# Values projected in the routing pass, slot lists built by VectorE beside four rounds, gate with tokens on partitions: one change to a fused attention and mixture-of-experts kernel

## The chip, the cores and the metric

The kernel runs on one core of a Trainium2 chip. The metric is the device time of one execution in microseconds, the median of several runs. All data is float32.

## The reference: what is computed

For 4096 tokens (4 sequences of 1024) of width H = 256:

```
xn  = layernorm(x)
out = x + attention(xn) + moe(xn)
attention: q, k, v = xn @ w.T, 16 heads of 16
  local  = causal linear attention with elu(q)+1, elu(k)+1, in chunks of 128 tokens
  coarse, fine = reads of four memories per head by elu(q)+1
  gprob  = sigmoid(relu(coarse @ eg_w1.T + b1) @ eg_w2.T + b2)      # one per token
  output = (gate*(gprob*fine + (1-gprob)*coarse) + (1-gate)*local) @ w_o.T
moe: logits = xn @ gate_weight.T (8 experts), softmax, top 2, weights renormalised
  y = sum over the 2 chosen experts of weight * swiglu_expert(xn), plus a shared swiglu expert
```

An expert is 176 wide, the shared one 352. A token's two experts are found first; then rows of `xn` are gathered expert by expert.

## The kernel before

**Tiles.** Tokens come in 32 tiles of 128 (`NTT`), four to a block (`NT = 4`), eight blocks (`NBLK`). `xnT` holds a block's normalised tokens with channels on partitions; every projection reads it. For the experts, the 8192 (token, choice) pairs are sorted by expert and packed into `NST = 71` slots of 128 rows, each slot belonging to one expert.

**Order.** Nothing is scheduled by the compiler: `manual_schedule` keeps the order in which Python calls the functions, and each engine runs its own instructions in that order. A *unit* is (weight, function, arguments). `mix` interleaves several lists of units in proportion to the weights, `split` cuts a list into parts of like weight, `run` emits. So a weight only places a unit; it is no time. The PSUM has the four banks of `quad` and a rotation of four single banks, `bank(...)`.

**Stages, in the order they are emitted (L1102 to L1152):**

1. *Routing*: a software pipeline over the blocks: `statistics` (VectorE), three steps later `normalize` (VectorE one tile, ScalarE three, then SP stores the block to `xns` in DRAM), one more step later `transpose_x` (TensorE, copied by ScalarE), one more `logits`. Only six blocks of `x` fit in SBUF (`AHEAD`), so the loads of blocks 6 and 7 are issued behind the stores of blocks 0 and 1. `logits` multiplies each token tile with 128 columns of `wvg` (values and gate weights side by side, 264 columns) and keeps the last eight. The queries of blocks 0 and 1 are projected here too. `route(0)` chooses the experts of the first half. After the loop SP copies `x` to `sums` in DRAM.
2. *Sorting and the head* (L1129 to L1144): one `mix` of `sorting` with block 0's keys and values, its shared expert, and attention rounds 0 and 1. `sorting` is `route(1)`, `sort`, `slots`, `weights`: VectorE chains on small tiles; then the slot lists: 22 batches of `invert` (one-hots of three columns of pairs: `places`, position within a slot, and `tiles`, number of the slot; GpSimd multiplies `tiles` with token numbers and with weights into `held`) each followed by `add_slots` (TensorE: `found += places.T @ held`); then `inverted` (writes `islot`, `wslot`) and `owners`.
3. *Rounds 2 to 29*: each is a `mix` of `attention_round(n)`, a quarter of the projections of a later block (`beside`: keys, values, queries, shared expert of blocks 1 to 7, spread over rounds 0 to 27), and 1/28 of `experts()` (`side`). A round scores and masks tile n (`scores`, `mask`), transposes and writes out tile n-2 (`output`), reads the memories (`memory`, `weigh`, `fine`), computes the gate of tile n-1 (`gate_hidden`, `gate_out`) and the local attention (`local`, `back`, `update`). A slot takes `fetch` (GpSimd gathers rows of `xns`, SP loads the weights), `expert_in`, `expert_hidden`, `expert_turn`, `expert_out`, and `put` (GpSimd issues a DMA that adds the result to `sums`).
4. *Tail*: rounds 30 to 33 with `totals`, which read `sums` back and write `out`.

**The gate before.** `gate_hidden` puts the 64 hidden channels on partitions (`w1` stationary, tokens streaming), ScalarE adds the bias and applies Relu, and `gate_out` multiplies by `w2` in one column on TensorE (L840) ahead of the Tanh.

Of the kernel before, what the change touches and what calls it, by code (L numbers as in the profile page):

```python
# [22 lines left out]
def linear_attention_moe_kernel(  # L23
# [51 lines left out]
    AHEAD = 6  # L75
# [10 lines left out]
    big = ctx.enter_context(tc.tile_pool(name="big", bufs=AHEAD))  # L86
# [13 lines left out]
    def bank(name):  # L100
        return ps_r.tile([P, 512], FP, tag="r", name=name)


    def load_x(blk):
        xb = big.tile([P, NT, H], FP, tag="tok", name=f"x_{blk}", bufs=AHEAD)
        nc.sync.dma_start(
            xb, x[blk * TB : (blk + 1) * TB, :].rearrange("(n p) h -> p n h", p=P)
        )
        st["x", blk] = xb

    for blk in range(AHEAD):
        load_x(blk)
# [18 lines left out]
    b1 = const.tile([HID, 1], FP, tag="b1", name="b1")  # L131
    nc.scalar.dma_start(b1, eg_b1)
    w2 = const.tile([HID, 1], FP, tag="w2", name="w2")
    nc.scalar.dma_start(w2, eg_w2)
# [169 lines left out]
    def normalize(blk):  # L304

        xb = st["x", blk]
        mv, rstd = st.pop(("norm", blk))
        shift = small.tile([P, NT], FP, tag="shift", name=f"shift_{blk}")
        nc.vector.scalar_tensor_tensor(
            shift, mv[:, :, 0], -1.0, rstd, ALU.mult, ALU.mult  # L310
        )
        xnT = io.tile([P, NC, TB], FP, tag="xnT", name=f"xnT_{blk}")
        st["xnT", blk] = xnT
        nc.vector.tensor_scalar(
            xb[:, NT - 1, :], xb[:, NT - 1, :], mv[:, NT - 1, 0:1], rstd[:, NT - 1 : NT],
            ALU.subtract, ALU.mult,
        )
        for i in range(NT - 1):
            nc.scalar.activation(
                xb[:, i, :], xb[:, i, :], AF.Identity,  # L320
                bias=shift[:, i : i + 1], scale=rstd[:, i : i + 1],
            )
        nc.sync.dma_start(
            xns[blk * TB : (blk + 1) * TB, :].rearrange("(n p) h -> p n h", p=P), xb
        )
        if blk + AHEAD < NBLK:
            load_x(blk + AHEAD)

# [13 lines left out]
    def logits(blk):  # L342

        xnT = st["xnT", blk]
        pl = bank(f"pl_{blk}").rearrange("p (i e) -> p i e", i=NT)
        for i in range(NT):
            for k in range(NC):
                nc.tensor.matmul(
                    pl[:, i, :], xnT[:, k, i * P : (i + 1) * P], wvg[:, k, H + E - P : H + E],
                    start=(k == 0), stop=(k == NC - 1),  # L350
                )
        nc.scalar.copy(lgs[:, blk * NT : (blk + 1) * NT, :], pl[:, :, P - E :])
# [134 lines left out]
    def invert(lo):  # L487
# [3 lines left out]
        if lo == 0:  # L491
            st["found"] = bank("found")
        n = min(3, 2 * NTT - lo)
        some = slice(lo, lo + n)
# [3 lines left out]
        tiles = ones_at[:, n * P : n * (P + NST)].rearrange("p (n s) -> p n s", s=NST)  # L498
        nc.vector.tensor_tensor(
            tiles, count[:, None, :NST].to_broadcast([P, n, NST]),  # L500
            lohi[:, 1, some, None].to_broadcast([P, n, NST]), ALU.is_equal,
        )
        nc.vector.tensor_tensor(
            places, count[:, None, :P].to_broadcast([P, n, P]),
            lohi[:, 0, some, None].to_broadcast([P, n, P]), ALU.is_equal,
        )
        held = exw.tile([P, 2 * H], FP, tag="wdn", name=f"held_{lo}")
        held = held[:, : n * 2 * NST].rearrange("p (n v s) -> p n v s", v=2, s=NST)
        for v, what in enumerate((token, two)):
            nc.gpsimd.tensor_mul(  # L510
                held[:, :, v], tiles, what[:, some, None].to_broadcast([P, n, NST])
            )
# [53 lines left out]

    def values(blk, i):
        xnT = st["xnT", blk]
        if i == 0:
            wide = att.tile([P, NT, NH * D1 + CW - D1], FP, tag="va", name=f"va_{blk}")  # L570
            nc.gpsimd.memset(wide[:, :, NH * D1 :], 0.0)
            va = wide[:, :, : NH * D1].rearrange("p i (h k) -> p i h k", k=D1)
            nc.gpsimd.memset(va[:, :, :, HD:D1], 1.0)
            st["va", blk] = va
            st["wide", blk] = wide
        pv = bank(f"pv_{blk}_{i}")
        for k in range(NC):
            nc.tensor.matmul(  # L578
                pv[:, :H], xnT[:, k, i * P : (i + 1) * P], wvg[:, k, :H],
                start=(k == 0), stop=(k == NC - 1),  # L580
            )
        nc.scalar.copy(
            st["va", blk][:, i, :, :HD],
            pv[:, :H].rearrange("p (h k) -> p h k", k=HD),
        )
# [239 lines left out]
    def gate_hidden(n):  # L825

        cT = st.pop(("cT", n))
        ph = bank(f"ph_{n}")
        for c in range(NC):
            nc.tensor.matmul(  # L830
                ph[:HID, :P], w1[:, c, :], cT[:, c, :], start=(c == 0), stop=(c == NC - 1)
            )
        h1 = tmp.tile([HID, P], FP, tag="h1", name=f"h1_{n}")
        nc.scalar.activation(h1, ph[:HID, :P], AF.Relu, bias=b1)
        st["h1", n] = h1

    def gate_out(n):

        pz = bank(f"pz_{n}")
        nc.tensor.matmul(pz[:, :1], st.pop(("h1", n)), w2, start=True, stop=True)  # L840
        prob = small.tile([P, 1], FP, tag="prob", name=f"prob_{n}")
        nc.scalar.activation(prob, pz[:, :1], AF.Tanh, bias=b2, scale=0.5)
# [166 lines left out]
    first_round, last_round = 2, 30  # L1009
# [12 lines left out]
    def run(units):  # L1022
        for _, f, *args in units:
            f(*args)

    def keys_values(blk):
        units = [(1024, project, blk, wk, c, False) for c in range(NC)]
        return units + [(512, values, blk, i) for i in range(NT)]
# [10 lines left out]
    def projections(blk):  # L1039

        units = keys_values(blk) + (queries(blk + 1) if blk + 1 < NBLK else [])
# [28 lines left out]
    def experts():  # L1070
        units = [(1, fetch, 0), (1, fetch, 1), (128, expert_in, 0)]
# [31 lines left out]
    for s in range(NBLK + 5):  # L1103
# [8 lines left out]
        if 0 <= s - 5 < NBLK:  # L1112
            routing += [(256, logits, s - 5)]
        if s == NBLK:
            routing += [(64, memories_by_group)]
        if s == NBLK + 1:
            routing += [(256, route, 0)]
        if NBLK <= s < NBLK + 2 * BPB:
            blk, c = divmod(s - NBLK, NC)
            routing += [(1024, project, blk, wq, c, True)]  # L1120
# [8 lines left out]
    sorting = [(2000, route, 1), (1800, sort), (100, shift_logits), (3200, slots)]  # L1129
    sorting += [(2400, weights)]  # L1130
    batches = list(range(0, 2 * NTT, 3))
    for k, lo in enumerate(batches):
        sorting += [(200, invert, lo)]
        sorting += [(400, add_slots, batches[k - 1])] if k else []
    sorting += [(400, add_slots, batches[-1]), (64, inverted), (1200, owners)]
    start = keys_values(0)
    start[4:4] = [(64, living), (64, mean_queries, 0), (64, gates_of_heads)]
    start += [(64, batch_weights, 0), (32, odd_keys, 0)]
# [3 lines left out]
    head = [u for n in range(first_round) for u in rounds[n]]  # L1142
    head = mix(head, shared(0) + [u for n in range(first_round) for u in beside[n]])
    run(mix(sorting, start + head))  # L1144
# [64 lines left out]
```

## Time and profile before

| | us |
|---|---|
| three runs | 776.08, 778.08, 779.90 |
| median of them | 778.08 |
| the profiled execution, its own time | 782.79 |
| its span, first to last instruction | 781.1 |

| engine | busy us | share of the span | instructions |
|---|---|---|---|
| PE (matmul) | 700.7 | 90% | 5268 |
| PEld (weight load) | 491.0 | 63% | 5268 |
| DVE (VectorE) | 426.1 | 55% | 1084 |
| ACT (ScalarE) | 273.8 | 35% | 707 |
| POOL (GpSimd) | 400.3 | 51% | 441 |

How to read it: a group's row has line, engine, operation, output<-inputs, shape, count, then busy time and the mean duration of one, then idle time of the engine just before it and what ended it. A float32 matmul is recorded as two instructions, so x4 in the chain stands for two calls. "Chain" is the work that ended last, followed back from the end. A stretch of the windows view gives, for 20 us, the busy time of each engine, the clock that TensorE was granted (1.00 is full) and the share of the DMA engines.

### The profile page before, as it was taken

The numbers are of one execution on the slowest core, as the hardware profiler recorded it, in microseconds if no ns is written. First come the engines' busy times: TensorE is split into PE (matmuls) and PEld (weight loads), VectorE is DVE, ScalarE is ACT, GpSimd is POOL, SyncE is SP. The second block draws the span as 40 slices with busy tenths as digits, with TensorE's granted clock in tenths as the row PEclk, the third lists the DMA queues.
The fourth block names the chain that finished last, engine by engine and source line by source line (L and its number), as shares of the span: only waits on it lengthen the run. The fifth ranks groups of instructions, "written<-read, shape, count | busy, mean of one in ns | idle before, by whom it ended". The sixth has DMA issues, their size and how long they took to land.

```text
span 781.1 us, 14630 instructions
## 1 busy us (share of the span) xinstructions
PE 700.7 (90%) x5268; PEld 491.0 (63%) x5268; DVE 426.1 (55%) x1084; ACT 273.8 (35%) x707; POOL 400.3 (51%) x441
## 2 busy tenths in 40 slices
PE   1798579499999999999999999999999999999965
PEld 0675356366676666666667667666766667767653
DVE  6536857445446744455536644554457555655553
ACT  2563002123443333433443343433443344334300
POOL 3100366506555656464546555556545646657576
PEclk9899689889999999999999999999999999999976
DMA  9554000234343453344444443443443444454285
GB/s 283 183 178 134 1 0 1 59 107 97 84 117 85 90 118 84 86 106 94 97 111 92 103 104 84 93 113 84 97 104 85 107 101 103 108 123 99 29 261 171
DMA packets 86373, 81.48 MB, mean 104 GB/s; under 512 B 7437, under 2 KB 83901, under 8 KB 86173
## 3 DMA queue, kind: packets, MB, share of 16 engines
q1 hardware_dynamic: 69661, 59.64, 26.5%
q0 software_dynamic: 13632, 18.62, 14.3%
q10 hardware_dynamic: 3008, 2.28, 0.9%
q8 instruction: 42, 0.69, 0.4%
q14 instruction: 30, 0.25, 0.1%
HBM read 62.56 MB, written 22.15 MB: 108 GB/s over the span
## 4 chain that ended last, share of the span: by engine, by line
PE 76%; DVE 7%; DMA 5%; POOL 4%; ACT 3%; issue 3%; SPq 0%; POOLq 0%; DVEq 0%; ACTq 0%
PE phe L968 12%; PE pye L991 8%; PE po L895 5%; PE psu L871 5%; PE pg L856 5%; PE quad L658 4%; PE pn L684 4%; PE po L899 3%; PE pv L578 3%; PE pq L550 3%; PE pk L550 3%; PE quad L770 3%; PE pxg L959 2%; PE pTe L982 2%; PE ph L830 2%
## 5 line engine op out<-in xcount | busy, mean ns | idle before, releaser
L1000 POOL DMA_INDIRECT sums<-y,islot x71 | 112.7, 1588 | 81.0 <-DMA sums<-y,islot 29.9
L792 POOL TENSOR_TENSOR cg<-coarse,gates 128x256 f32<-128x256 f32 x32 | 23.7, 742 | 165.1 <-DVE coarse L785 164.9
L968 PE MATMUL phe<-wgu,xgT 128*128 128x352 f32 x284 | 100.9, 478 | 1.1 <-ACT hTe L984 0.9
L665 DVE TENSOR_TENSOR sT<-quad,causal 128x512 f32<-128x512 f32 x128 | 80.2, 682 | 14.3 <-PE pk L736 6.5
L933 POOL DMA_INDIRECT xg<-xns,islot x71 | 71.3, 1005 | 15.9 <-issue 8.8
L991 PE MATMUL pye<-wdn,hTe 88*128 88x256 f32 x284 | 76.6, 392 | 1.8 <-ACT oT L822 1.0
L968 PEld LDWEIGHTS phe<-wgu,xgT 128*128 128x128 f32 x284 | 49.9, 191 | 25.3 <-issue 5.3
L810 POOL TENSOR_TENSOR fm<-fm 128x512 f32<-128x512 f32 x32 | 43.6, 1363 | 36.5 <-DVE prob L843 23.1
L974 DVE SCALAR_TENSOR_TENSOR the<-the,phe 128x176 f32<-128x176 f32 x71 | 23.8, 335 | 69.6 <-ACT the L973 66.8
L991 PEld LDWEIGHTS pye<-wdn,hTe 88*128 88x128 f32 x284 | 49.5, 189 | 15.1 <-issue 5.5
L995 ACT ACTIVATE y<-pye,wslot 128x256 f32<-128x256 f32 x71 | 33.6, 473 | 58.6 <-PE pye L991 55.7
L895 PE MATMUL po<-wd,h 128*128 128x256 f32 (+1 forms) x192 | 49.2, 394 | 0.0
L973 ACT ACTIVATE the<-phe 128x176 f32<-128x176 f32 x71 | 22.5, 318 | 74.5 <-PE phe L968 72.5
L871 PE MATMUL psu<-xnT,wu 128*128 128x512 f32 (+1 forms) x96 | 47.6, 620 | 0.0
L856 PE MATMUL pg<-xnT,wg 128*128 128x512 f32 (+1 forms) x96 | 47.0, 613 | 0.7 <-ACT nT L691 0.7
L799 DVE TENSOR_TENSOR fm<-quad,rw 128x512 f32<-128x512 f32 x64 | 42.0, 682 | 0.0
L863 DVE SCALAR_TENSOR_TENSOR th<-th,pg 128x512 f32<-128x512 f32 (+1 forms) x24 | 16.4, 684 | 43.8 <-ACT th L862 39.6
L876 DVE SCALAR_TENSOR_TENSOR h<-th,psu 128x512 f32<-128x512 f32 (+1 forms) x24 | 16.5, 686 | 42.9 <-PE psu L871 42.2
L961 ACT COPY xgT<-pxg 128x256 f32<-128x256 f32 x71 | 26.5, 373 | 37.1 <-PE pxg L959 18.3
L895 PEld LDWEIGHTS po<-wd,h 128*128 128x128 f32 (+1 forms) x192 | 36.1, 200 | 4.3
L558 DVE SCALAR_TENSOR_TENSOR sqT<-pq,eq 128x512 f32<-128x512 f32 x16 | 11.1, 692 | 50.8 <-ACT eq L556 50.7
L563 DVE SCALAR_TENSOR_TENSOR skT<-pk,ek 128x512 f32<-128x512 f32 x16 | 11.1, 691 | 49.8 <-ACT ek L556 47.1
(195 smaller groups left out, 1510.2 us busy)
## 6 DMA issues: line engine op xcount, KB each, us to landing
wgu<-in_w_gate_dram SPq DMA_DIRECT2D x71, 176.0 KB
wgu<-in_w_up_dram SPq DMA_DIRECT2D x71, 176.0 KB
wdn<-in_w_down_dram SPq DMA_DIRECT2D x71, 176.0 KB
x<-in_x_dram SPq DMA_DIRECT2D x8, 512.0 KB
xns<-x SPq DMA_DIRECT2D x8, 512.0 KB
sums<-in_x_dram SPq DMA_DIRECT2D x8, 512.0 KB
part<-sums SPq DMA_DIRECT2D x14, 256.0 KB
out_dram<-acc SPq DMA_DIRECT2D x14, 256.0 KB
```

Source lines behind the costliest of these rows:

```text
L550: nc.tensor.matmul(pq, w[:, k, c * P : (c + 1) * P], xnT[:, k, :], start=(k == 0), stop=(k == NC - 1),)
L665: nc.vector.tensor_mul(sT, quad[:, g, :].rearrange("p (c t) -> p c t", t=P), causal[:, None, :].to_broadcast([P, NC * 2, P]),)
L799: nc.vector.tensor_mul(fm[:, c].rearrange("p g m (r k) -> p g (m r) k", k=HD), quad[:, :, c * KM + KX + KN : (c + 1) * KM].rearrange("p g ...
L810: nc.gpsimd.tensor_add(fm[:, :, 0:2, :], fm[:, :, 0:2, :], fm[:, :, 2:4, :])
L856: nc.tensor.matmul(pg[:n, :], wg[:, k, f * P : f * P + n], xnT[:, k, :], start=(k == 0), stop=(k == NC - 1),)
L871: nc.tensor.matmul(pu[:n, :], wu[:, k, f * P : f * P + n], xnT[:, k, :], start=(k == 0), stop=(k == NC - 1),)
L895: nc.tensor.matmul(po[:, :H], st["h", blk, f][:k, tok], wd[:k, f, :], start=(f == 0), stop=False)
L933: nc.gpsimd.indirect_dma_start(out=xg, out_offset=None, in_=xns, in_offset=bass.IndirectOffsetOnAxis(ap=islot[:, j : j + 1], axis=0),)
L968: nc.tensor.matmul(ph[:, : 2 * F], xgT[:, k, :], wgu[:, k].rearrange("p g f -> p (g f)"), start=(k == 0), stop=(k == NC - 1),)
L991: nc.tensor.matmul(py[:, :H], hT[:, f, :], wdn[:, f, :], start=(f == 0), stop=(f == 1))
L995: nc.scalar.activation(y, py[:, :H], AF.Copy, scale=wslot[:, j : j + 1])
L1000: nc.gpsimd.indirect_dma_start(out=sums, out_offset=bass.IndirectOffsetOnAxis(ap=islot[:, j : j + 1], axis=0), in_=st.pop(("y", j)), in_of ...
```

## The change

Five edits that hang together:

- *Values in the routing.* `logits` is gone; `values` runs in its place for all eight blocks, two token tiles at a time, with all 264 columns of `wvg` into `quad`. ScalarE copies 256 columns to the values and eight to `lgs`. The values overwrite the block's own `x` tile, which is made wider (`VW`), so there are eight such tiles and all eight loads are issued at once (no `AHEAD`); the copy into it must wait for the block's store to `xns`. `keys_values` becomes `keys`. The queries of blocks 0 and 1 leave the routing.
- *normalize*: VectorE two tiles, ScalarE two (was one and three).
- *invert*: per column three `tensor_scalar` on VectorE: `places` by is_equal, and each half of `held` by is_equal and multiply in one instruction. GpSimd has no part in it.
- *Order*: sorting is mixed with the queries of blocks 0 and 1, block 0's keys and shared expert only. Then rounds 0 to 3 run with `beside` and the slot lists (`owners` first, `add_slots` two batches behind `invert`), and `fetch` 0 and 1 at their end. `first_round` is 4, so the experts are spread over 26 rounds instead of 28.
- *Gate*: tokens on partitions. The coarse tile is stationary and `w1` (64 columns) streams; VectorE adds the bias, then does Relu, multiply by `w2` and the sum in one instruction with an accumulator. The one-column matmul and ScalarE's Relu are gone.

```diff
-        xb = big.tile([P, NT, H], FP, tag="tok", name=f"x_{blk}", bufs=AHEAD)
+        wide = big.tile([P, NT, VW], FP, tag="tok", name=f"x_{blk}")
+        xb = wide[:, :, :H]
...
-    for blk in range(AHEAD):
+        st["wide", blk] = wide
+    for blk in range(NBLK):
         load_x(blk)
...
-    def logits(blk):
...
-                    pl[:, i, :], xnT[:, k, i * P : (i + 1) * P], wvg[:, k, H + E - P : H + E],
...
+    def values(blk, pair):
+        xnT, wide = st["xnT", blk], st["wide", blk]
+        if pair == 0:
+            st["va", blk] = wide[:, :, : NH * D1].rearrange("p i (h k) -> p i h k", k=D1)
+        va = st["va", blk]
+        tiles = slice(2 * pair, 2 * pair + 2)
+        for i in range(2 * pair, 2 * pair + 2):
+            for k in range(NC):
+                nc.tensor.matmul(
+                    quad[:, i, : H + E], xnT[:, k, i * P : (i + 1) * P], wvg[:, k, :],
+                    start=(k == 0), stop=(k == NC - 1),
+                )
+        nc.scalar.copy(va[:, tiles, :, :HD],
+            quad[:, tiles, :H].rearrange("p i (h k) -> p i h k", k=HD))
+        nc.scalar.copy(lgs[:, blk * NT + 2 * pair : blk * NT + 2 * pair + 2, :],
+            quad[:, tiles, H : H + E])
+        nc.gpsimd.memset(va[:, tiles, :, HD:D1], 1.0)
+        nc.gpsimd.memset(wide[:, tiles, NH * D1 :], 0.0)
...
-        nc.vector.tensor_tensor(tiles, ..., ALU.is_equal)
-        nc.vector.tensor_tensor(places, ..., ALU.is_equal)
...
-            nc.gpsimd.tensor_mul(
-                held[:, :, v], tiles, what[:, some, None].to_broadcast([P, n, NST])
-            )
+        for k in range(n):
+            j = slice(lo + k, lo + k + 1)
+            nc.vector.tensor_scalar(places[:, k], count[:, :P], lohi[:, 0, j], None, ALU.is_equal)
+            for v, what in enumerate((token, two)):
+                nc.vector.tensor_scalar(
+                    held[:, k, v], count[:, :NST], lohi[:, 1, j], what[:, j],
+                    ALU.is_equal, ALU.mult,
+                )
...
-                ph[:HID, :P], w1[:, c, :], cT[:, c, :], start=(c == 0), stop=(c == NC - 1)
...
-        nc.scalar.activation(h1, ph[:HID, :P], AF.Relu, bias=b1)
+                ph[:, :HID], cT[:, c, :], w1[:, c, :], start=(c == 0), stop=(c == NC - 1)
...
+        nc.vector.tensor_add(h1, ph[:, :HID], b1)
+        nc.vector.scalar_tensor_tensor(h1, h1, 0.0, w2, ALU.max, ALU.mult, accum_out=z)
...
-        nc.tensor.matmul(pz[:, :1], st.pop(("h1", n)), w2, start=True, stop=True)
...
-    first_round, last_round = 2, 30
+    first_round, last_round = 4, 30
...
-        units = [(1, fetch, 0), (1, fetch, 1), (128, expert_in, 0)]
+        units = [(1000, lambda: None), (128, expert_in, 0)]
...
-            routing += [(256, logits, s - 5)]
+            routing += [(1056, values, s - 5, p) for p in range(NT // 2)]
...
-        if s == NBLK + 1:
+        if s == NBLK + 2:
             routing += [(256, route, 0)]
-        if NBLK <= s < NBLK + 2 * BPB:
-            blk, c = divmod(s - NBLK, NC)
-            routing += [(1024, project, blk, wq, c, True)]
...
+    sorting = [(2400, route, 1), (600, sort), (3600, slots), (100, shift_logits), (2400, weights)]
+    start = [u for blk in range(BPB) for u in queries(blk)] + keys(0)
+    start[3:3] = [(64, living), (64, gates_of_heads)]
+    start += [(64, mean_queries, 0), (64, batch_weights, 0), (32, odd_keys, 0)]
+    run(mix(sorting, start + shared(0)))
...
+    lists = [(600, owners)]
+    for k, lo in enumerate(batches):
+        lists += [(400, invert, lo)]
+        lists += [(768, add_slots, batches[k - 2])] if k > 1 else []
+    lists += [(768, add_slots, lo) for lo in batches[-2:]]
+    lists += [(64, inverted), (10, fetch, 0), (10, fetch, 1)]
+    lists = split(lists, first_round)
+    for n in range(first_round):
+        run(mix(rounds[n], beside[n], lists[n]))
```

## The prediction, on record before the changed kernel ran

> **What bounds the kernel now.** First the page: is one engine full, and when?
>
> ```profile
> span 781.1 us, 14630 instructions
> PE 700.7 (90%) x5268; PEld 491.0 (63%) x5268; DVE 426.1 (55%) x1084; ACT 273.8 (35%) x707; POOL 400.3 (51%) x441
> ...
> PE   1798579499999999999999999999999999999965
> ```
>
> From the ninth slice to the 38th TensorE is full: there, time saved on it is time saved. The gaps lie in the first 156 us and the last 40. The windows view of 20 us (PE, PEld, DVE, ACT, POOL, clock, DMA, GB/s) sizes them:
>
> ```profile
> 40.00:60.00 20.00, 20.00 (x117) 14.19 (x116) 6.68 (x23) 11.97 (x26) 0.00 (x0) 1.00 0.58 188
> 60.00:80.00 20.00, 14.98 (x77) 9.38 (x75) 14.54 (x53) 6.19 (x15) 0.00 (x0) 0.91 0.36 111
> 80.00:100.00 20.00, 12.81 (x74) 8.49 (x75) 15.58 (x33) 0.59 (x1) 8.85 (x12) 0.66 0.00 1
> 140.00:160.00 20.00, 9.45 (x64) 6.72 (x64) 6.16 (x20) 3.38 (x7) 8.82 (x13) 0.73 0.37 106
> 200.00:220.00 20.00, 19.02 (x154) 13.20 (x153) 9.64 (x24) 8.95 (x23) 9.15 (x11) 1.00 0.35 82
> ```
>
> While the slot lists are made, TensorE is short of work and its clock falls to 0.66. The groups give prices, and the chain shows what holds it last before the experts start:
>
> ```profile
> L348 PE MATMUL pl<-wvg,xnT 128*128 128x128 f32 x128 | 18.9, 311 | 0.0
> L840 PE MATMUL pz<-w,h 64*128 64x1 f32 x64 | 12.1, 257 | 0.7 <-ACT h L834 0.7
> L518 PE MATMUL found<-held,ones 128*128 128x142 f32 x128 | 23.5, 329 | 11.4 <-POOL held L510 11.2
> L503 DVE TENSOR_TENSOR ones<-count,lohi 128x384 f32<-128x384 f32 x21 | 16.4, 781 | 0.0
> L314 DVE TENSOR_SCALAR x<-x,mv,rstd 128x256 f32<-128x256 f32 x8 | 3.2, 406 | 0.3 <-issue 0.3
> L596 DVE TENSOR_SCALAR qr<-ones,qsum x8: 276/286/815, 67.8 to 584.9; 128x128 f32<-128x128 f32 x8
> ...
> 145.74 4.36 issue
> ...
> 151.22 4.25 DMA xg<-xns,islot
> 155.61 0.66 PE pxg L959 x2
> ```
>
> (L596's numbers are least, median and largest ns.) TensorE waits 11 us for `held`, then stands from 146 to 155.6 for the first gather.
>
> **What the Trainium skill says.** "TensorE: Matmul & The Clock Gate", "Back-to-back issue gap": a matmul costs its streamed columns, with a floor of about 60 cycles for 1 to 64 columns. The trace agrees in kind: `tot` with 5 columns takes 0.36 us for x4 in the chain, where 512 take 1.72. The same page, "What's actually happening": idle windows of some 3.4 us halve the clock; the 0.66 above agrees. "VectorE: DVE Perf Modes", "The perf-mode tier table", gives float32 `tensor_scalar` double speed; the trace does not: 276 ns for 128 elements (L596), 406 for 256 (L314), one element per ns and some 145 fixed. "SBUF — State Buffer", "SBUF: two separate sides": VectorE and GpSimd can lock each other out of a shared port; L596 is 276 alone and 815 at worst, which fits.
>
> **The change, part by part.**
>
> *Logits into values.* In the chain one block's logits take 1.79 us at full clock (x16), so 14.3 us go. Eight columns on 256 add 1/32 of the values: a block's values are four times 0.89 (chain, L578 x4 in the full rounds), 3.56, so 0.11 a block, 0.9 in all. Net -13.4 of TensorE.
>
> *Routing with the values.* The start is as before: x_0 lands at 5.7, its transposes start at 16. Per block TensorE now has transposes 1.0 and values 3.67; ScalarE two normalised tiles 1.06, two transposes 1.04, value copies 2 x 0.59 (price of the 512-wide nT, L691) and logits 2 x 0.19: 3.7, below 4.7, so TensorE sets the pace. New wait: the copy into the `x` tile needs the store to `xns` done. Behind it on ScalarE are the next normalise and copies; on GpSimd the memsets (about 0.2 each) and the last rstd. Before, that store went out at 16.9 and landed at 21.3; now two loads of 512 KB are ahead of it on SP and in the DMA engines, so I take 24 to 25. From there later stores are ahead of need. TensorE from 25: seven blocks of values 25.7, five of transposes 5.0, some cold clock 2: **58 us** at the end of routing, where before it was 57.6, with 6.9 us of queries and none of the values. Bounds: 54 (no wait at all), 64 (each copy 1 us late).
>
> *Sorting stage.* TensorE: four q and two k at 1.72, six shared at 1.72, 1 for the rest, 22 us. VectorE: q and k 4.0, shared 3.7, `route(1)` 3.3, `sort` to `weights` 11.0, gates and living 2.2, batch weights 3.2: 27. The order makes them alternate: first queries reach VectorE 3 us after the start (matmul, two ScalarE passes), the keys stand behind `pp`, which waits for `sort` (4), shared tiles wait for banks that VectorE frees late (2 to 3). I take 37 (bounds 29, 44): **95**.
>
> *Rounds 0 to 3 with the lists.* GpSimd's 30 us (L510) go, VectorE's 27.5 (L499, L503) become 192 `tensor_scalar`. 128 elements cost 0.276; two in a row in the trace take 0.48, so 0.204 each. 71 elements I set at 0.205 alone and 0.135 in a row. A column is 0.204 + 2 x 0.135 = 0.474, 64 of them 30.3 (all single: 0.686, 43.9). Other VectorE work per round: masks 2.5, weigh 1.7, fine 1.25, back 1.2, update 0.4, gate and o 1.35: 8.4; four rounds less one gate 32.2, block 1's projections 6.3, owners and inverted 2.6: 41. For the port I add 6: GpSimd works 5.4 a round, 22 in all, and 40% of VectorE's time is lists, of which I count most (bounds 0, 18). Sum **77**. TensorE has 27 (rounds), 17.8 (block 1 without values), 15.5 (`found`, 64 x 0.243): 60. So VectorE, not GpSimd, is the bound here: **172**. Cover for the lists is gone on VectorE, but `add_slots` two batches later keeps TensorE from waiting on each.
>
> *First gather.* inverted, 1.2 on GpSimd, 4.25 of DMA: 6 to 7 us, against 3.5 of round 4 ahead of the first `expert_in`. The 4.36 "issue" before was `owners` on VectorE; it now runs first. 4 us stay: **176**.
>
> *Gate.* `pz` is 0.32 in the chain, x32. `ph` falls from 0.58 to between 0.36 (`tot`) and 0.58: 0.42 taken. 0.48 a round. VectorE gains 0.55 a round (128x64 from PSUM about 0.2, then 0.2 and accumulator read 0.08) at 10.6 busy of 20: hidden in the full rounds. Behind the add wait `fine` and the experts' products; `ph` follows `memory` within about 2 us, while `weigh` takes 1.7.
>
> *Full rounds.* Before: first pxg 155.6 to last pye 732.6 (chain), 577. Experts: phe 1.30, pye 0.97, pTe 0.33, pxg 0.33, 2.93 x 71 = 208. Projections 5.35 a round (21.4 a block) x 26 = 139. Left 230 over 28 rounds, 8.2. After: 26 x (8.2 - 0.48) + 24 x (5.35 - 0.91) + 208 = 201 + 107 + 208 = **516**. Ends at 692. Experts per round 2.73 instead of 2.54. TensorE's other waits in the old rounds sum to about 12 us; I keep them.
>
> *Tail.* 781.1 - 732.6 = 48.5, unchanged: span **740.5**. normalize's shift and the smaller PSUM use lie beside other work.
>
> Outside the span 1.7 (782.79 - 781.1): 742.2 for such an execution, which stood 4.7 above the median; so **737.5**, -5.2%.
>
> **Rivals.**
>
> *Lists hidden.* VectorE's overlap is better and TensorE paces: rounds 0 to 3 at 65, sorting at 32: 720.5. For it: in 120 to 140 us before, both ran at 18.4 to 18.5 of 20. Against: 77 of VectorE's work is a sum without waits.
>
> *Lists dear.* No overlap (+13.6) and more of the port (+6): 757. For it: 815 in L596, 0.37 and 0.71 in L499's same operation.
>
> *Slots keep their pace, slower than before.* The experts may be paced by GpSimd's chain: each put (L1000, 1.59) waits for the one before to land, and gathers and products queue behind. If a slot stays at 577/71 = 8.13 us, the 71 take 577 from 176: span 801.5, so 798.5. It decides from 7.84 a slot ((781.1 - 176 - 48.5)/71) upward; I forecast 7.27. For it: GpSimd is idle 30 us for such landings. Against: in the tail a put lands after 2.33 to 3.71, a turnaround of 4 to 5.3, and TensorE hardly waits for experts.
>
> That the change doesn't do what it says: only if the store wait held each value copy; that is the 64 above.
>
> **How the numbers follow.** Forecast 0.58, hidden 0.16, dear 0.18, slots 0.08. The range 719 to 761 takes in the first three with their bounds. About 0.5% is what a measurement of this kernel can tell from no change: faster 0.90, within 0.02, slower 0.08.
>
> **What would show it.** Routing's last matmul at 54 to 64; first expert transpose near 176 with four rounds done; VectorE over 90% busy between 95 and 172 with no GpSimd in the lists; 7.3 us a slot; the tail 48. Wrong if TensorE waits for `xns` stores beyond block 0, if lists take over 97 us, or if rounds 4 to 29 take over 530.

## The result, and the profile after

The changed kernel takes 782.44 us (median of 7 runs, 781.99 to 783.73), the kernel before, run beside it, 778.66 (776.08 to 779.90): ratio 1.006, 95% interval 1.0044 to 1.0077. It is slower by 0.6%, where 5% faster was forecast. The profiled execution took 782.04 us, with a span of 780.3 us.

The page of the changed kernel, busy times and slices:

```profile
span 780.3 us, 14382 instructions
...
PE 673.2 (86%) x5076; PEld 468.3 (60%) x5076; DVE 476.5 (61%) x1336; ACT 256.6 (33%) x659; POOL 371.8 (48%) x413
...
PE   1786767577899999999999999999999999999664
...
DVE  5622398699756766565567655655667566656462
```

TensorE has 27.5 us less to do (700.7 before), and yet the end comes no sooner: its full stretch now starts at the twelfth slice in place of the ninth. Work was taken out where TensorE was full, and gaps were opened where it was not. The windows view of the changed kernel has the same stretches as the forecast showed of the kernel before (PE, PEld, DVE, ACT, POOL, clock, DMA, GB/s):

```profile
40.00:60.00 20.00, 17.35 (x89) 13.51 (x86) 4.00 (x14) 11.62 (x29) 1.47 (x16) 1.00 0.49 158
60.00:80.00 20.00, 13.35 (x42) 8.16 (x43) 5.87 (x23) 6.34 (x15) 0.00 (x0) 0.90 0.47 145
80.00:100.00 20.00, 14.68 (x31) 5.89 (x30) 8.23 (x32) 5.33 (x10) 0.00 (x0) 0.84 0.00 0
140.00:160.00 20.00, 12.56 (x94) 8.59 (x94) 14.01 (x52) 2.99 (x6) 0.73 (x1) 0.74 0.01 1
200.00:220.00 20.00, 17.09 (x139) 11.30 (x138) 13.01 (x37) 4.59 (x11) 8.98 (x10) 0.91 0.40 109
```

Between 60 and 100 us no engine is busy for more than three quarters of the time. Between 140 and 160 us VectorE, forecast to be over 90% busy, works 14.0 of 20 and TensorE 12.6: neither is full, so they wait for each other.

Set against the forecast's own steps, by the spans of the profiled executions:

| step | forecast, us | measured, us | difference |
|---|---|---|---|
| routing with the values, to its last matmul | 58 | 68.05 | +10.0 |
| sorting stage, to the owners | 37 | 43.2 | +6.2 |
| rounds 0 to 3 with the lists | 77 | 99.9 | +22.9 |
| first gather | 4 | 4.1 | +0.1 |
| first expert transpose to last expert matmul | 516 | 510.3 | -5.7 |
| tail | 48.5 | 54.8 | +6.3 |
| span | 740.5 | 780.3 | +39.8 |

From the kernel before to the changed one, first expert transpose at 155.6 and then at 215.2: the head is 59.6 us longer. The full rounds are 66.7 shorter, the tail 6.3 longer. That leaves the two profiled spans 0.8 apart; the profiled execution of before stood 4.1 above the median of its seven runs and that of after 0.4 below its own, so the medians differ by 3.8 the other way.

**Routing.** The timeline of TensorE in the changed kernel, one block of 5.6 us (start, length, count, and in brackets the idle time before it and what ended it):

```profile
28.57 1.04 PE L337 MATMUL pt<-ident,x 128*128 128x128 f32 x8
29.48 2.05 PE L354 MATMUL quad<-wvg,xnT 128*128 128x264 f32 x8
32.33 2.05 PE L354 MATMUL quad<-wvg,xnT 128*128 128x264 f32 x8 [0.79 <-ACT lgs L362]
34.21 1.04 PE L337 MATMUL pt<-ident,x 128*128 128x128 f32 x8
```

And of ScalarE at the same time:

```profile
31.61 0.59 ACT L358 COPY x<-quad 128x512 f32<-128x512 f32 x1 [0.24 <-issue]
32.10 0.18 ACT L362 COPY lgs<-quad 128x16 f32<-128x16 f32 x1
```

The second pair's matmuls (32.33) start when ScalarE has copied the first pair's logits out (32.10 and 0.18). The second pair goes into other banks of `quad` than the first, and still it waits: both lie in one PSUM tile, and the wait is on the tile. The group of the changed kernel adds these waits up:

```profile
L354 PE MATMUL quad<-wvg,xnT 128*128 128x264 f32 x128 | 33.6, 407 | 7.2 <-ACT lgs L362 7.2
```

7.2 us, nine times 0.8. The store wait that the forecast feared is not among what TensorE waits for there: the first values start at 22.9, ahead of the 25 that the forecast took.

**Rounds 0 to 3.** What TensorE waits for in the changed kernel from 111.2 to 211.2 us (sum, times, longest):

```profile
PE quad L759 <- DVE sT L654: 11.8, 2, 6.2
PE quad L647 <- DVE prob L832: 4.8, 2, 2.8
PE found L527 <- DVE held L518: 4.7, 2, 3.7
```

The longest of these waits, in TensorE's timeline:

```profile
139.36 1.96 PE L527 MATMUL found<-held,ones 128*128 128x142 f32 x6 [1.01 <-DVE held L518]
147.54 1.52 PE L759 MATMUL quad<-mem,sqT 32*128 32x170 f32 x16 [6.22 <-DVE sT L654]
148.99 3.02 PE L559 MATMUL pq<-xnT,wq 128*128 128x512 f32 x4
```

And VectorE's, of which the lines of the lists between 144.3 and 146.2 are left out:

```profile
143.07 1.28 DVE L654 TENSOR_TENSOR sT<-quad,causal 128x512 f32<-128x512 f32 x2
...
146.21 1.28 DVE L654 TENSOR_TENSOR sT<-quad,causal 128x512 f32<-128x512 f32 x2
...
153.34 0.69 DVE L567 SCALAR_TENSOR_TENSOR sqT<-pq,eq 128x512 f32<-128x512 f32 x1 [5.86 <-ACT eq L565]
```

TensorE stands 6.2 us for the last mask (its memory products go into `quad`, from which the masks read the scores), and in VectorE's queue that mask lies behind columns of the lists. Then TensorE has to make the memory products and a query at a lowered clock (3.02 us where the forecast's row had 1.72), ScalarE two passes over it, and now VectorE stands 5.9 us for that query. The sum of VectorE's work held no such turns.

### The profile page after: what moved, and what is told of

Read it like the earlier page. It is cut to its first block, busy times and chain, and to the rows that moved or that the text cites. A ratio compares the mean times of both kernels' runs of the same rounds, so it can differ in the third digit from the quotient of the medians.

```text
span 780.3 us, 14382 instructions
## 1 busy us (share of the span) xinstructions
PE 673.2 (86%) x5076; PEld 468.3 (60%) x5076; DVE 476.5 (61%) x1336; ACT 256.6 (33%) x659; POOL 371.8 (48%) x413
## 5 line engine op out<-in xcount | busy, mean ns | idle before, releaser
L781 POOL TENSOR_TENSOR cg<-coarse,gates 128x256 f32<-128x256 f32 x32 | 24.1, 752 | 184.7 <-DVE coarse L774 184.7
L957 PE MATMUL phe<-wgu,xgT 128*128 128x352 f32 x284 | 99.1, 472 | 2.5 <-PE pTe L971 2.1
L884 PE MATMUL po<-wd,h 128*128 128x256 f32 (+1 forms) x192 | 53.1, 417 | 1.6 <-ACT cT L811 0.9
L962 ACT ACTIVATE the<-phe 128x176 f32<-128x176 f32 x71 | 22.5, 317 | 75.3 <-PE phe L957 75.3
L884 PEld LDWEIGHTS po<-wd,h 128*128 128x128 f32 (+1 forms) x192 | 38.6, 210 | 9.9 <-ACT cT L811 1.8
L354 PE MATMUL quad<-wvg,xnT 128*128 128x264 f32 x128 | 33.6, 407 | 7.2 <-ACT lgs L362 7.2
L759 PE MATMUL quad<-mem,sqT 32*128 32x170 f32 x512 | 28.9, 341 | 11.8 <-DVE sT L654 11.8
L834 DVE SCALAR_TENSOR_TENSOR o<-diff,prob,loc 128x256 f32<-128x256 f32 x32 | 36.2, 1131 | 4.4 <-DVE prob L832 1.0
```

Source lines behind the costliest of these rows:

```text
L354: nc.tensor.matmul(quad[:, i, : H + E], xnT[:, k, i * P : (i + 1) * P], wvg[:, k, :], start=(k == 0), stop=(k == NC - 1),)
L834: nc.vector.scalar_tensor_tensor(o, st.pop(("diff", n)), prob, st.pop(("base", n)), ALU.mult, ALU.add)
L884: nc.tensor.matmul(po[:, :H], st["h", blk, f][:k, tok], wd[:k, f, :], start=(f == 0), stop=False)
L957: nc.tensor.matmul(ph[:, : 2 * F], xgT[:, k, :], wgu[:, k].rearrange("p g f -> p (g f)"), start=(k == 0), stop=(k == NC - 1),)
```

## The experiments

Each ratio is to the kernel before on the same chip. "After" is the changed kernel, with ratio 1.006.

**The gate alone, on the kernel before** (gate_only): of the whole change only the biases and weights as rows, `gate_hidden` and `gate_out`.

```
-        nc.tensor.matmul(pz[:, :1], st.pop(("h1", n)), w2, start=True, stop=True)
+        nc.vector.tensor_add(h1, ph[:, :HID], b1)
+        nc.vector.scalar_tensor_tensor(h1, h1, 0.0, w2, ALU.max, ALU.mult, accum_out=z)
```

> The kernel before with the gate edit alone. Theory (the gate edit pays in the full rounds, and the head is what lost it): some 0.45 us less of TensorE a round, 28 full rounds and 4 others, 12 to 15 us less: 764 to 767. Rival (VectorE's added work and its waits for the hidden layer eat it): within 3 us of the 778.7 before.

Measured: 776.59 us, ratio 0.9988 (0.9973 to 1.0002). The full rounds of its profile are 566, 11 shorter than the 577 of the profile of before, but the head is 2.2 longer and the tail 3.6 longer. With the 4.1 us by which that profile of before stood above its median, next to nothing is left; some of the 11 may be that slow execution. The tail's loss is the gate's (see below). Of the head's 2.2 us, 1.8 are there when the last logits are multiplied (59.3 in place of 57.5), ahead of any gate, so they are not its work on VectorE.

**Lists as before** (lists_pool): after, with the old `invert`, wide comparisons on VectorE and products on GpSimd.

```
...
+        nc.vector.tensor_tensor(
...
-            nc.vector.tensor_scalar(places[:, k], count[:, :P], lohi[:, 0, j], None, ALU.is_equal)
...
-                nc.vector.tensor_scalar(
-                    held[:, k, v], count[:, :NST], lohi[:, 1, j], what[:, j],
...
+            nc.gpsimd.tensor_mul(
+                held[:, :, v], tiles, what[:, some, None].to_broadcast([P, n, NST])
```

> The changed kernel with the slot lists' one-hots as before (VectorE two comparisons a batch, GpSimd the products). Theory (rounds 0 to 3 last as long as VectorE's work there, and the lists are 0.65 us a column on it): VectorE gives up 64 x 0.65 plus some 5 us of stalls and takes back 27: rounds 0 to 3 shorten by 12 to 18 us, 765 to 770. Rival (their length is the ring of scores, masks, memory reads and fine, whatever VectorE does in between): within 4 us of 782.4.

Measured: 763.51 us, ratio 0.9804 (0.9764 to 0.9843), 19 us below after. From the owners' reduction to the last slot weights it takes 78.6 us in place of 98.7; the full rounds keep their length (510.5). The new lists are dearer than the old by 20 us, and nearly all of it shows at the end. VectorE stands idle for 14 us of this stretch with the old lists too, against 11.8 with the new: what went is work, 22.5 us of it, and not the waits.

**Values through single banks** (values_banks): after, each tile's values into a bank of the ring of four, with copies of its own.

```
-                    quad[:, i, : H + E], xnT[:, k, i * P : (i + 1) * P], wvg[:, k, :],
+                    pv[:, : H + E], xnT[:, k, i * P : (i + 1) * P], wvg[:, k, :],
...
```

> The changed kernel with each token tile's values in a single PSUM bank of the rotation instead of in quad, copied tile by tile. Theory (in the routing TensorE and ScalarE take turns on quad, since the waits are on all of it: 0.79 us per pair): no wait of TensorE for the copy of logits, routing ends 6 to 9 us earlier, 774 to 776. Rival (the stores to xns, or ScalarE itself, set the pace): routing's end moves by less than 2 us.

Measured: 770.07 us, ratio 0.9894 (0.9863 to 0.9926), 12 us below after, more than the theory had. The group's wait falls to nothing, and the last value matmul starts at 58.4 (67.8 in after):

```profile
L355 PE MATMUL pv<-wvg,xnT 128*128 128x264 f32 x128 | 31.5, 404 | 0.0
```

The edit also copies one tile at a time in place of two, so it does not tell the shared tile from the size of the copy; the 0.79 us in after's timeline, ended each time by the copy out of the other pair, speaks for the tile.

**Places twice** (places_twice): after, each of the 64 comparisons of 128 elements issued twice into the same place.

> The changed kernel with every comparison for places issued twice (64 more of 128x128 on VectorE, the result unchanged). Theory (VectorE is the bound of rounds 0 to 3): 64 x 0.2 = 13 us longer there, 792 to 796. Rival (VectorE has slack there): under 4 us.

Measured: 800.81 us, ratio 1.029 (1.0252 to 1.0328): +18 us for 64 instructions, 0.28 each. VectorE's work does set the length of these rounds. That each cost more than a start every 0.20 us comes of the probe itself: in the trace the second comparison waits for a semaphore that the first raises when it is done, since both write the same place, and so starts 0.31 later.

**Both repairs** (pool_banks): lists_pool and values_banks together.

> The changed kernel with both repairs together: the one-hots made as before (wide comparisons on VectorE, products on GpSimd), and the values through single banks. If the lists and the routing cost independently, in the stages where they lie, the two gains add: 782.4 - 18.9 - 12.4 = 751 us. If one of them hides behind the other, or GpSimd's products come to bound rounds 0 to 3 once the routing is shorter, 757 or more.

Measured: 748.41 us, ratio 0.9659 (0.9626 to 0.9691). The gains add: by the ratios the two runs above would make 0.9638 together, which is within the interval. In its profile the last value matmul starts at 58.0, the lists' rounds take 77.5 and the full rounds 510.1. Its window over the lists' rounds:

```profile
100.70:178.40 77.70, 64.49 (x584) 47.84 (x585) 64.72 (x140) 13.98 (x31) 47.84 (x67) 0.91 0.05 15
```

beside that of after, which opens 1 us ahead of the owners' reduction where the other opens at it:

```profile
111.20:211.20 100.00, 74.42 (x585) 53.80 (x586) 88.22 (x291) 14.39 (x32) 19.11 (x24) 0.80 0.05 13
```

The same matmuls (584 and 585) take 10 us less at the better clock, 0.91 in place of 0.80, and VectorE has 22.6 us less to do once both windows open alike, though GpSimd has 29 more.

**What the list instructions cost** (held_probe): after, with two more in each column.

```
+            nc.vector.tensor_scalar(
+                places[:, k], count[:, :P], lohi[:, 0, j], 1.0, ALU.is_equal, ALU.mult
+            )
+            nc.vector.tensor_scalar(held[:, k, 0], count[:, :NST], lohi[:, 1, j], None, ALU.is_equal)
```

> The changed kernel with two more tensor_scalar in each column of the lists, each writing where the next one writes again: a 128-element one with two operations (is_equal with a scalar from a tile, times the constant 1), and a 71-element one with is_equal alone. If the second operation costs the time that my price of 0.135 us lacked, the 71 elements with one operation take about 205 ns and start 0.135 apart, and the 128 with two about 305. If the fixed part of this form is simply longer and the row length doesn't rule, the 71-element one takes 250 or more. 128 more instructions at 0.2 to 0.28 each: 808 to 818 us in all.

Measured: 816.81 us in one run. One column in VectorE's timeline (L516 is one operation on 128, L517 two with a constant, L520 one on 71, L522 two with scalars from tiles):

```profile
115.20 0.28 DVE L516 TENSOR_SCALAR ones<-count,lohi 128x128 f32<-128x128 f32 x1
115.52 0.29 DVE L517 TENSOR_SCALAR ones<-count,lohi 128x128 f32<-128x128 f32 x1
115.72 0.25 DVE L520 TENSOR_SCALAR held<-count,lohi 128x71 f32<-128x71 f32 x1
116.00 0.32 DVE L522 TENSOR_SCALAR held<-count,lohi 128x71 f32<-128x71 f32 x1
116.24 0.31 DVE L522 TENSOR_SCALAR held<-count,lohi,two 128x71 f32<-128x71 f32 x1
116.46 0.28 DVE L516 TENSOR_SCALAR ones<-count,lohi 128x128 f32<-128x128 f32 x1
```

The medians are 279 ns for 128 elements with one operation, 286 with a second one by a constant, 250 for 71 elements with one, and 310 for 71 with two scalars from tiles. So 57 elements fewer save 29 ns, half a nanosecond each, and the second scalar from a tile adds 60. Both of the forecast's sizes were off: the row length matters less than it took, and the second scalar costs more. Starts lie 0.20 to 0.24 apart where the place is new, and 0.28 to 0.32 where the instruction writes over the one before, for whose semaphore it then waits.

**The gate as before, in the new order** (gate_old): after, with the old gate.

> The changed kernel with the gate as before (hidden units on partitions, a second matmul for the logit). If the new gate saves TensorE 0.45 us a round in the full rounds and only some of it returns in the tail, this is 7 to 9 us slower: 790 us, with the stretch from the first expert transpose to the last expert matmul 11 to 12 longer and the tail 3 to 4 shorter. If the new gate is worth nothing in all, as the run with the gate alone on the kernel before had it: 781 to 784.

Measured: 785.64 us, ratio 1.011 (1.008 to 1.0141), 3 us above after. The size lies between the two theories and the parts fit the first: the full rounds are 519.9 (+9.6) and the tail is 51.2 (-3.6); the head is 2.3 shorter, for its lists' rounds take 95.9 in place of 98.7. What TensorE waits for in the tail of after, for the output of the gate:

```profile
PE poT L809 <- DVE o L834: 9.6, 2, 5.7
```

and with the old gate, where TensorE waits for other things instead in part, 14.4 in all in place of 20.0:

```profile
PE poT L809 <- DVE o L834: 5.0, 2, 2.5
```

**The gate's bias on TensorE** (gate_bias): pool_banks, with a one-row matmul for the bias, so that VectorE's one instruction reads PSUM.

```
+        nc.tensor.matmul(ph[:, :HID], ones[0:1, :], b1[0:1, :], start=False, stop=True)
-        nc.vector.tensor_add(h1, ph[:, :HID], b1)
-        nc.vector.scalar_tensor_tensor(h1, h1, 0.0, w2, ALU.max, ALU.mult, accum_out=z)
+        nc.vector.scalar_tensor_tensor(h1, ph[:, :HID], 0.0, w2, ALU.max, ALU.mult, accum_out=z)
```

> The changed kernel with both repairs, and the gate's bias added by a one-row matmul into the hidden units' bank, so that VectorE's add goes and its one remaining instruction reads PSUM instead of two tiles in SBUF. If the new gate gave so little because its VectorE instruction waits for GpSimd's adds (724 ns median for 64 elements, 225 when GpSimd is idle), the instruction falls to 200 to 250 ns and the whole takes 744 to 746 us. If TensorE's own work is all that counts in the full rounds, the added matmul of some 0.1 us a round makes it 749 to 752.

Measured: 758.73 us, ratio 0.9769 (0.9721 to 0.9817), 10 us above pool_banks (8.5 by the ratio), more than either theory. The VectorE instruction does what the first theory said. In after it is this (after the count: least, median and largest ns):

```profile
L825 DVE SCALAR_TENSOR_TENSOR h<-h,w x32: 225/724/927, 157.8 to 768.5; 128x64 f32<-128x64 f32 x32
```

In 29 of its 32 turns GpSimd multiplies the coarse tile by the gates (L781) at the same time, from some 0.08 us before its start to 0.08 before its end, as here:

```profile
723.33 0.72 POOL L781 TENSOR_TENSOR cg<-coarse,gates 128x256 f32<-128x256 f32 x1 [4.22 <-DVE coarse L774]
723.41 0.72 DVE L825 SCALAR_TENSOR_TENSOR h<-h,w 128x64 f32<-128x64 f32 x1
```

The one turn with no GpSimd work beside its start takes 225 ns. In gate_bias, with the added matmul ahead of it:

```profile
L823 PE MATMUL ph<-b,ones x64: 270/294/318, 133.7 to 744.2; 1*128 1x64 f32 x64
L826 DVE SCALAR_TENSOR_TENSOR h<-ph,w x32: 211/214/225, 137.8 to 745.1; 128x64 f32<-128x64 f32 x32
```

The median falls from 724 to 214 ns, though L781's product runs beside it in 29 turns as before; in four of them it even started first, and the instruction took 225 at most. In the full rounds this gains nothing. The matmul with one row and 64 columns takes two passes of 294 ns, 0.59 a round; the full rounds go from 510.1 to 521.6, 0.44 a round. There TensorE's passes are the price, and half a microsecond of VectorE is free. In the tail, where TensorE is not full, the profile is shorter: 50.4 in place of 53.1.

**Slots dealt by the other work of a round** (experts_even): after, with rounds 28 and 29 taking fewer slots.

> The changed kernel with the slots dealt out by the other work of each round, so that rounds 28 and 29, which have no projections, take 1.9 slots each in place of 2.7. If the tail grew because the last slots end 3.7 us apart while a put takes 4.4 to 5 us to land, the puts no longer trail: from the last expert matmul to the landing of the last put 7 to 9 us in place of 12.8, and 777 us in all. If the end is set by the last rounds' attention and gate instead, 781 to 784, with the time only moved.

Measured: 778.53 us, ratio 1.0035 (1.0016 to 1.0054), 4 us below after, but 2 by the ratio, and the two intervals overlap. The tail is 53.7 in place of 54.8, and the last put is still issued 8.4 us after the last expert matmul (8.1 in after). So the edit did not bring the puts forward, and the run does not test the theory about them. What its profile gains is in the full rounds, 506.9 in place of 510.3.

**No slots in rounds 28 and 29** (experts_early): after, the 71 slots in rounds 4 to 27.

```
-    side = split(experts(), last_round - first_round)
+    side = split(experts(), last_round - 2 - first_round) + [[], []]
```

> The changed kernel with the slots dealt to rounds 4 to 27 alone, so that rounds 28 and 29 are attention without experts. If the end waits for GpSimd's puts, which trail the last expert matmul by 8 us and hold up every load of the sums, the two rounds cover them: 773 to 777 us, with the last put landing less than 5 us after the end of round 29's matmuls. If the last rounds' attention and gate set the end, 780 to 784, the same work in another order.

Measured: 785.67 us, ratio 1.0059 (1.0033 to 1.0084), the same as after. Its last expert matmul ends at 718.0, 7.5 us earlier, and its span is 780.5. The loads of the sums start at 729 in place of 738, and the puts are no longer on the chain that ended last; the last rounds' matmuls and VectorE steps are there in their place. But rounds 28 and 29 also come 12 us and more later here (the last `o` of the two starts at 738.5 in place of 725.9), since their slots went ahead of them. So the run shows a second path of about the same length, and not that the puts cost nothing in after.

**Keys ahead of the sort** (keys_first): after, the routing of the second half, then all four queries and both keys, then the rest mixed.

```
...
-    run(mix(sorting, start + shared(0)))
+    run(sorting[:1] + start[:4] + start[6:8])
+    run(mix(sorting[1:], start[4:6] + start[8:] + shared(0)))
```

> The changed kernel with all four query and both key projections ahead of the sort in every engine's order, so that no key stands behind the sort's own matmul on TensorE. If the waits for each other cost the sorting stage its 6 us above my sum, the owners start at 105 to 107 in place of 111.2 and the whole takes 777 us. If VectorE's own work bounds the stage, 781 to 784.

Measured: 779.26 us, ratio 1.0034 (1.0004 to 1.0064), which is not clear of after's. The stage gains 1.9 us of the 5 expected (the owners' reduction starts at 110.3 in place of 112.2). VectorE's timeline:

```profile
87.09 0.42 DVE L435 TENSOR_TENSOR sort_work<-pick 128x256 f32<-128x256 f32 x1
93.72 0.69 DVE L852 SCALAR_TENSOR_TENSOR th<-th,pg 128x512 f32<-128x512 f32 x1 [6.21 <-ACT th L851]
```

The keys no longer wait, and a wait of 6.2 us for the first shared tile has come in their place, since TensorE starts that tile late. Moved, not removed.

**Round 0 beside the sort** (round0_mixed): pool_banks, round 0 and its projections mixed into the sorting stage, the lists in rounds 1 to 3.

> The changed kernel with both repairs, and round 0 with its projections put beside the sort, the lists over rounds 1 to 3 alone. If the sorting stage is long by waits of the engines for each other (VectorE works 25 of its 42 us there, TensorE 30), round 0 fills them: the stage from the end of the values to the owners goes from 42 to about 50, the lists' rounds from 77.5 to 65, 743 us in all. If the stage is as long as the work that is in it, round 0 only moves: 747 to 750.

Measured: 751.03 us, ratio 0.9674 (0.9618 to 0.9731), no gain over pool_banks. The owners' reduction starts 19.1 us later (119.8 in place of 100.7), and the lists' rounds take 64.2 in place of 77.5, 13.3 less. So round 0 does not fit into the waits of the sort. That it stands in the queues between the sort's steps and lengthens them is the likely reason; no run tests it.

**Lists one column at a time** (by_column): after, the same instructions in units of a third.

> The changed kernel with the lists handed to the order of work one column at a time (0.65 us of VectorE) instead of three (2 us), the same instructions. If the 12 us that VectorE is idle and the 12 that TensorE waits for masks in rounds 0 to 3 come of masks and projections standing behind bursts of list work, rounds 0 to 3 fall from 100 to about 93 and the whole to 775 us. If what they wait for is further away than a burst (projections that a later mask releases), no gain: 780 to 784.

Measured: 787.91 us, ratio 1.0069 (1.0047 to 1.0091), the same as after. The two waits for masks are there unchanged (11.8 us, the longest 6.2), and the lists' rounds take 96.2 us in place of 98.7 where 7 less were hoped for. So the length of the bursts does not make these waits. That the amount of list work between two masks does fits lists_pool, where TensorE waits 3.7 us for masks, but no run shows it alone.

**All four edits** (all_four): pool_banks with experts_even and keys_first.

> The changed kernel with four edits together: lists as before, values through single banks, slots dealt by the rounds' other work, keys ahead of the sort. If the gains stay apart as the first two did: 748.4 - 3.9 - 3.2 = 741 us. If the last two only worked on waits that the first two already took away: 747 to 750.

Measured: 751.36 us where the kernel before took 781.5 on that chip: ratio 0.9602 (0.958 to 0.9624). Against pool_banks, whose runs are of another chip (the kernel before took 776.7 there), the ratio is 0.6% lower and the intervals just miss each other; in the profiles neither its head (first expert transpose 183.6, pool_banks 182.8) nor its full rounds (513.4, 510.1) are shorter. So all_four has the lowest ratio, 4% below the kernel before, but what the last two edits add to it stays unproven. Nearly all of the gain is in the two repairs.

## Why the prediction was wrong

**What held.** The first gather (4 forecast, 4.1 measured) and the full rounds (516, 510.3) came close to what was worked out, the rounds partly by luck: the gate gave 9.6 of the 12.5 us that it had in them, and other terms came out some 8 lower, for which no cause was found. A slot now takes 510.3/71 = 7.19 us, so the rival that slots keep 8.13 falls. The head decided.

**Failed step: rounds 0 to 3, the sum of 77.** It is the largest term, +22.9 us, and it failed in two places.

*The price of a column.* "71 elements I set at 0.205 alone and 0.135 in a row ... A column is 0.204 + 2 x 0.135 = 0.474." The group view of after, from 111.2 to 211.2:

```profile
L518 DVE TENSOR_SCALAR held<-count,lohi 128x71 f32<-128x71 f32 x64 | 23.6, 369 | 0.0
L518 DVE TENSOR_SCALAR held<-count,lohi,two 128x71 f32<-128x71 f32 x64 | 19.6, 306 | 0.0
L516 DVE TENSOR_SCALAR ones<-count,lohi 128x128 f32<-128x128 f32 x64 | 19.3, 302 | 0.0
```

71 elements took 306 and more, not 205, and a column starts every 0.65 us (113.09, 113.73 and 114.38 in VectorE's timeline). With overlaps taken out, list instructions fill 48.6 us of VectorE, where 30.3 and 6 for the port were forecast: +12.3. The price is what failed: 64 columns at 0.65 are 41. The 6 for the port held: 12 of the 192 instructions took much longer than their median (375 to 1357 ns), each beside one of GpSimd's, some 5.6 us in all.

The reading behind the price was wrong: 276 ns for 128 elements and 406 for 256 were put on one line, "one element per ns and some 145 fixed", but the first row multiplies by one scalar from a tile and a constant, the second uses two from tiles. Rows of the same form give another line: 279 at 128 and 250 at 71 with one operation, 308 at 71 and 406 at 256 with two scalars from tiles. Each is about 0.5 ns an element, over 215 and 270 fixed. That is half of the 1 ns that the forecast read. So its remark that the trace does not show what the Trainium skill says, "VectorE: DVE Perf Modes", "The perf-mode tier table", was itself wrong: the double speed for float32 `tensor_scalar` fits these rows, over a larger fixed part. At 71 elements it is mostly the fixed part that one pays, and it is paid 192 times where the wide comparisons pay it 44 times. The forecast's own rival, the lists dear at 43.9 and the port 12, was near in its price (55.9 with the port), but at 757 us still far from the result.

*The waits.* The forecast added up VectorE's work and took the sum as the length of the rounds. VectorE was idle for 11.8 of the 100 us (88.2 busy): the queries wait for TensorE, which waits for masks, which wait for list columns. 48.6 of lists and 42.9 of other work, less some 3 in which instructions overlap, and 11.8 make the 100. `add_slots` two batches later kept TensorE from the lists (4.7 us in all), as forecast; it did nothing for the masks that share VectorE's queue. The clock, 0.74 between 140 and 160, made TensorE's part of each turn longer. Such idle time is no fault of the new lists (lists_pool has 14 of it); the forecast left it out of its sum.

**Failed step: routing, "so TensorE sets the pace", 58.** The work was right: in pool_banks and values_banks the last value matmul starts at 58.0 and 58.4. What failed is that ScalarE's 3.7 below TensorE's 4.7 lets TensorE set the pace only if the two overlap. Through one `quad` they took turns in part, nine times 0.8 us. The forecast named a wait for the copy (the store to `xns`, bounds to 64) and passed over the one that the PSUM tile made. Cost: +10.0. values_banks ends its routing 9.4 earlier than after, and takes 12 less in all.

**Failed step: sorting, "I take 37".** Measured 43.2, within the bounds of 29 to 44 but at their end. VectorE's 27 was about right (24.0 busy), TensorE's 22 was 30.8 busy, at clock 0.88. In keys_first and round0_mixed two other orders mostly moved the waits; which order would do better was not found.

**Failed step: tail, "48.5, unchanged".** +6.3 us. The chain that ended last runs, before and after, through the landing of the last put, for which the loads of the sums wait (start, length; before, then after):

```profile
738.21 3.71 DMA sums<-y,islot
733.61 4.66 DMA sums<-y,islot
```

It lands 9.3 us after the last expert matmul before, and 12.8 after: 3.5 of the 6.3. From there to the end it is 39.2 and 42.0: the other 2.8.

The gate is in both: gate_old has 11.1 and 40.1, 3.6 less in all, and gate_bias, whose VectorE part is short, has 11.1 and 39.3 where pool_banks has 11.5 and 41.6. In the tail nothing else fills TensorE while VectorE adds, multiplies and reads the accumulator. The forecast had VectorE's part of the gate "hidden in the full rounds", rightly, and left out that the first four rounds and the last ones have no such cover. The last 2.7 us, between gate_old and before, stay open; most of it is the later landing of the puts (11.1 against 9.3), which no run here brings forward by itself. The tails of the other runs with the new gate lie between 51.8 and 54.8 (experts_early apart), so a microsecond in such a sum means little.

**Mis-sized: the gate.** 0.48 us a round was forecast, 9.6/26 = 0.37 came in the full rounds. `pz` went, with 12.1 us busy, but `ph` with operands exchanged saves little: 18.8 us busy over all rounds in place of 20.8, 0.06 a round, where 0.16, 5 us in all, was forecast. VectorE's part was sized at 0.55 a round and took 1.0: 0.21, 0.72 and 0.08. The 0.72 is a wait inside the instruction: the Trainium skill, "SBUF — State Buffer", "Who interferes with whom", says that a VectorE instruction with two inputs in SBUF contends with a GpSimd one that reads SBUF. The trace agrees: with two SBUF inputs 711 to 927 ns beside GpSimd's product and 225 without it, with one from PSUM 211 to 225. The net between the two spans, 3.7 us, is what is left of 9.6 after 3.6 in the tail and 2.3 in the head.

**The wrong side.** None of the rivals was this one. The one that ended slower needed the slots; the case that came had routing and lists beyond their upper bounds (68 against 64; 99.9 against 96.6, the rival's 77 + 13.6 + 6), the sorting stage near its own, and a tail that had none, 45 us together. The bounds had been drawn one step at a time, from work, and those of the routing and the lists left out that engines wait in turn.

## What to carry to other kernels

When work moves to an engine that also makes something others wait for in every round, add up not only its work but also the turns: what stands behind the new instructions in its queue, and who then stands idle. Take the price of a short instruction only from a row of the same form (operations, scalars from tiles, where its inputs lie), since at 71 elements most of it is fixed (some 215 of 250 ns). And a saving on the full engine counts only where it is full: look for the rounds at both ends that have no cover.

## What was not expected of the hardware

- `tensor_scalar` on float32 in SBUF: 250 ns for 71 elements and 279 for 128 with one operation; a second operation by a constant adds 7 ns, by a second scalar from a tile 60.
- Such instructions of VectorE start 0.20 to 0.24 us apart, less than the 0.25 to 0.31 that each takes. One that waits for the semaphore of the one before it, because it writes the same place, starts 0.28 to 0.32 after it (held_probe).
- A matmul of one row by 64 columns takes 294 ns a pass, not less than one of 128 rows by 64 columns (275).
- `scalar_tensor_tensor` on 64 elements: 724 ns median with both inputs in SBUF while GpSimd multiplies, 225 without that, 214 with one of them in PSUM.
